# A four-block graph and state-space kernel: tokens by indirect transfers, leaky ReLU by the absolute value, a select by position on GpSimd, a fourth lane

## The chip, the cores and the metric

The kernel runs on one core of one Trainium2 chip. The core has TensorE (PE, with its weight loads shown apart as PEld), VectorE (DVE), ScalarE (ACT), GpSimd (POOL) and SyncE (SP), each with an in-order queue of its own, and 16 DMA engines. The metric is the time of one execution on the device in microseconds; lower is better.

## The reference, cut to what matters

The input x is 64 batches of 256 tokens of 256 features, in float32. Four residual blocks follow each other, each on a layer norm of x. `before` and after compute the same thing.

```
# block 1: two graph attentions (the second under adj), with MLPs between
e   = leaky_relu(f1[:, :, None] + f2[:, None, :], 0.2)
e   = where(adj > 0, e, -9e15)                 # second attention only
h'  = elu(softmax(e) @ h)
# block 2: the 127 tokens of a batch with the largest weight go through an FFN
w         = x @ wr + br
idx       = top_k(w, 128)[:127]
y         = (gelu(x[idx] @ w1 + b1) @ w2 + b2) * w[idx]
x         = x + scatter(y at idx, else 0)      # 'x' on the right: normalized x
# block 3: graph attention under adj, with -inf outside it
# block 4: Mamba-2 over one chunk of 256 positions
L     = exp(cs[l] - cs[s]) for s <= l, else 0  # per head, cs = cumsum(dt * A)
Y     = ((C @ B^T) * L) @ (x * dt), then gate, norm, two projections
```

Block 2 is added to x again after the layer norm, as in each block.

## The kernel before

**Tiling.** A group is two batches: 512 tokens, in four chunks of 128 partitions. There are 32 groups (n). A tile of x for one group is `xt`, 128 x 4 x 256. All matmuls are float32; the trace shows two records for a matmul and one for a transpose.

**Lanes.** The work is written as Python generators that issue a few instructions and then `yield`. Such a generator is a lane: `a` is the first block (`gnn0`, 55 steps), `b` the second and third (`ffn0` and `gnn1`, 57 steps), `c` the fourth (`ffn1`, 87 steps), `d` the second half of the first group's first block, `e` and `f` the two halves of the last group's fourth block (78 steps each), and `w` the preparation of weights. The order of instructions on all engines is that in which the steps are called: L1038 to L1048 walk three strings of letters. `FIRST` starts the pipeline, `ORDER` is walked 29 times, each pass taking one lane `a`, one `b` and one `c` of different groups through all its steps, and `LAST` empties it. A letter whose lane may not begin yet does nothing (`is_there`, L1021); what is left after `LAST` is stepped in turn (L1046 to L1048). `e` and `f` may begin when all groups have passed `b`.

**scores** (L422) turns f1 and f2 into unnormalized attention. f2 is spread over the partitions by four transposes into PSUM (`fb`), the row maximum gives the shift `nm`, ScalarE computes leaky ReLU by `Prelu` with f1 as bias, four instructions of 128x256, then `Exp` with the shift as bias and the row sum accumulated in `den`. VectorE takes the reciprocal and GpSimd scales e (L473). `turned` (L476) then transposes e on TensorE. It is called three times per group.

**Token choice** (L597). `wc` is each token's weight. `wrow` spreads it over the partitions, and two VectorE instructions per chunk count the larger ones (`tie`), which is the token's `rank`. `pick` (L628) is a 0/1 matrix of 128 tokens by 128 ranks. TensorE selects the tokens by multiplying with it (`psel`, L635), transposes it (`pt`, L645) and, after the FFN, brings the result back by multiplying with its transpose (`po`, L695). VectorE adds it to xn with the weight wc (L702), GpSimd adds that to xt (L705).

**The decay matrix** (L805 to L826). A row of cs goes through DRAM (`csd`) and is spread over 128 partitions by a DMA of SP into E (L809). E has 384 columns for each batch: the first 256 positions against the first 128, and the last 128 against the last 128; the first and the third 128 are the blocks on the diagonal (`diag`). For each head VectorE takes the minimum with cs of the partition (L820), which makes everything above the diagonal exp(0) = 1, ScalarE takes the exponential (L826), and VectorE multiplies by `cb` (L899), which is C B^T times `tri3` (L891), ones on and below the diagonal and zeros above. So the zeros come from tri3.

**Other names in the prediction.** `pp`, `pz`, `ph`, `py`, `u`, `pa`, `pd`, `pn`, `pb`, `pss`, `pst`, `pr` are PSUM tiles of the matmuls in the lanes; all PSUM tiles share eight buffers (L235). `mm` (L251) and `tr` (L254) are helpers, so nearly all TensorE records have one of these two lines. The convolution is one ScalarE and three VectorE instructions per 128 channels (L841, L845), followed by tanh and a product (`silu`, L850, L851). `power` (L264) is the inverse root of the variance on GpSimd.

Of the kernel before, what the change touches and what calls it, by code (L numbers as in the profile page):

```python
# [8 lines left out]
F32 = mybir.dt.float32  # L9
I32 = mybir.dt.int32  # L10
BF16 = mybir.dt.bfloat16
# [10 lines left out]
    "dwddadadwaaadawdaaddadaddaaaaadddaaddaaaaddaddaddadaaadaddaddwawdaaaaaaadddadddawdaaaaadadaadaddbaba"  # L22
    "aaabaaaabbaawaaaabwaabaaaaababbbaabbbwababababbbbabaaaabaabaawabababbaaaaabbbaaabbbbabbbaababbababab"
    "baababbbaaaabbabbbabbbaaacwccaababcaababbaabcaaabaaabacabbabbbbbaaabaabaabcbcabaabwbbaacabbaabawabca"
    "bbbab"
)
ORDER = (
    "cAaaccbbbbbbacabaccccbccaabacccabcbccabaacbccacabcaaaacacacbcccccbcacabcccbcaaacacbbccccccacaaccbcac"
    "cbacacabccabcccbcbBabccaccbcccabbcacaacbaccacbcbaacbcbbcbcababcbbcbCccbbbbaacaacabcaabbcbbabbbbbccc"
)  # L30
LAST = (
    "ececefefceecbbceccbbcbffbbbccfcbbfceccebbfcccbefccbcbeceebfcccecccecccceccfbccbcecccbccbeeccbefceccf"
    "ccccccfeeebbccecccfecffffcccfbffebcccbfbceffbccbcccefebbcefcccfceeebcbccccbfefccbcccbfbffcbbccccbcbb"
    "cfceefcbfbbcfefcbbcffbfecccbfcbfefbbbfbfbccffeeeebffbeccccfffebbfebbefbecfcbccccccbcbbcbffcccbeeceec"
    "ebfecbbbbcebffcceccbccccbeccebccececbbefcccffecfccffccfecfebcebceeceecebcffbcfeccfffcfecfeccefcececc"
    "cfe"
# [4 lines left out]
def kernel(ctx: ExitStack, tc: tile.TileContext, a: dict, out: bass.AP):  # L41
# [52 lines left out]
    tri3 = cons("tri3", P, 3 * P)  # L94
    nc.gpsimd.memset(tri3, 1.0)
    for blk in (0, 2):
        nc.gpsimd.affine_select(
            out=tri3[:, blk * P : (blk + 1) * P],
            in_=tri3[:, blk * P : (blk + 1) * P],
            compare_op=ALU.is_ge,  # L100
            fill=0.0,
            base=0,
            pattern=[[1, P]],
            channel_multiplier=-1,
        )

# [13 lines left out]
    ranks = cons("ranks", P, P)  # L120
    with tc.tile_pool(name="first", bufs=1) as first:
        iota_i = first.tile([P, P], I32, tag="iota_i", name="iota_i")
        nc.gpsimd.iota(iota_i, pattern=[[1, P]], base=0, channel_multiplier=0)
        nc.vector.tensor_copy(ranks, iota_i)
    nc.vector.memset(ranks[:, KK:P], -1.0)
# [75 lines left out]
    for t, ap in ((dtb, a["L1_ffn_dt_bias"]), (negA, a["L1_ffn_A_log"])):  # L201
# [28 lines left out]
        "xn": 2, "pk": 3, "v": 2, "g": 4,  # L230
# [6 lines left out]
    def tiled(pool, shape, tag, name, bufs):  # L237
        return pool.tile(list(shape), F32, tag=tag, name=name, bufs=bufs)
# [4 lines left out]
    def sm(tag, *shape, bufs=4):  # L243
        return tiled(small, shape, tag, tag, bufs)

    def sized_sm(tag, n, most, *rest, bufs=4):

        return sm(tag, P, most, *rest, bufs=bufs)[:, :n]
# [39 lines left out]
    def made_ready():  # L288
# [19 lines left out]
        nc.vector.tensor_scalar(mask1, adj, 0.0, -1e37, ALU.is_le, ALU.mult)  # L308
# [31 lines left out]
        yield  # L340
        for t in (b1h, conv_w, conv_b, W_in[:, :, :DI]):
            nc.vector.tensor_scalar(t, t, 0.5, None, ALU.mult)
# [23 lines left out]
    def sized(G, own=None):  # L366
# [12 lines left out]
        def columns(tag, name, most=512):  # L379
            t = wide(lambda tag, name: t512(tag, name) if most == 512 else tiled(t2, (P, most), tag, name, 4), tag, name)  # L380
            return t[:, (own or 0) * N : (own or 0) * N + T]
# [40 lines left out]
        def scores(f1, f2, mask, strict, tag):  # L422
# [3 lines left out]

            yield
            fb = psum("fb")
            for c in range(C):
                tr(fb[:, tok(c)], f2(c).to_broadcast([P, P]), ident)  # L430
            halves = [slice(h * N, (h + 1) * N) for h in range(2)]
            es = [t512(tag, "e") for b in range(G)]
            rows = [fb[:, b * N : (b + 1) * N] for b in range(G)]
            top = sized_sm("top", C, 4)
            if mask is None:
                most = sized_sm("most", G, 2)
                nc.vector.tensor_reduce(most, fb[:, :T].rearrange("p (b j) -> p b j", b=G), AX.X, ALU.max)
                for c in range(C):
                    nc.vector.tensor_scalar(
                        top[:, c : c + 1], most[:, c // 2 : c // 2 + 1], f1(c), -1.0, ALU.add, ALU.mult  # L440
                    )
            else:
                most = sized_sm("topm", C, 4)
                for c in range(C):
                    e = es[c // 2][:, halves[c % 2]]
                    nc.vector.tensor_tensor_reduce(
                        e, rows[c // 2], mask[:, c % 2, :], 1.0, -3e38, ALU.add, ALU.max, most[:, c : c + 1]
                    )
                for c in range(C):
                    nc.vector.tensor_scalar(  # L450
                        top[:, c : c + 1], most[:, c : c + 1], f1(c), -1.0, ALU.add, ALU.mult
                    )
            yield
            nm = sized_sm("nm", C, 4)
            nc.vector.scalar_tensor_tensor(nm, top, ALPHA, top, ALU.mult, ALU.min)
            den = sized_sm("den", C, 4)
            for c in range(C):
                e = es[c // 2][:, halves[c % 2]]
                nc.scalar.activation(e, rows[c // 2] if mask is None else e, AF.Prelu, bias=f1(c), alpha=ALPHA)
            yield  # L460
            for c in range(C):
                e = es[c // 2][:, halves[c % 2]]
                nc.scalar.activation(e, e, AF.Exp, bias=nm[:, c : c + 1], accum_out=den[:, c : c + 1])
            yield
            if strict:

                nc.vector.scalar_tensor_tensor(den, nm, 1e30, den, ALU.is_lt, ALU.mult)
# [614 lines left out]
```

## Time and profile before

| | us |
|---|---|
| median of 3 runs (lowest, highest) | 3652.24 (3652.19, 3652.80) |
| the profiled execution's own time | 3653.81 |
| its span, first to last instruction | 3652.1 |
| mean granted TensorE clock | 0.99 |
| DMA: bytes moved, share of 16 engines | 150.89 MB, 12.1% |

The page gives busy shares, the span in 40 slices, and groups of instructions; the trace behind it can be asked for stretches of time, for the instructions of one engine in order, and for what a waiting instruction waited for. Since matmuls overlap, the mean duration of one (379 ns for 256 columns) is longer than its share of the time, and a stretch of TensorE work is better read from the start of one group of matmuls to the start of the next. Groups that the change touches:

| line, engine | what, per instruction | count | mean ns |
|---|---|---|---|
| L820 DVE | minimum of E's diagonal blocks, 128x512 | 248 | 885 |
| L899 DVE | E times cb, 128x768 | 248 | 988 |
| L891 DVE | cb times tri3, 128x384 | 64 | 547 |
| L628 DVE | pick, 128x128 | 128 | 297 |
| L439, L450 DVE | top, 128x1 | 384 | 205 to 207 |
| L455 DVE | nm, 128x4 | 94 | 157 |
| L459 ACT | Prelu, 128x256 | 384 | 475 to 526 |
| L463 ACT | Exp with sum, 128x256 | 384 | 516 |
| L473 POOL | e times 1/den, 128x256 | 384 | 505 |
| L702 DVE | result of the FFN times wc plus xn, from PSUM, 128x256 | 128 | 476 |
| L715 DVE | two-input product in SBUF, 128x256 | 256 | 423 |
| L97 POOL | select by position, 128x128, once per block | 2 | 296 |

### The profile page before, as it was taken

To read this page: it belongs to the slowest core of one execution; us is meant where nothing else is said; L and a number is where in the kernel's file an instruction comes from. 1 tells how busy PE (TensorE), PEld (TensorE's weight loads), DVE (VectorE), ACT (ScalarE), POOL (GpSimd) and SP (SyncE) were. 2 spreads that over 40 slices of the span, in tenths; PEclk is the share of its full clock that TensorE was granted. 3 is DMA by queue.
4 is the path that set the end of the run, shared out by engine and by line. 5 is a ranking of instruction groups with operands and counts; after the bars stand their busy time and mean duration, and the time that the engine had idled before them with its cause. 6 is when DMAs were issued, how large, how long until landed. Compare 5 with 4: busy or idle time off the path is not lost.

```text
span 3652.1 us, 50662 instructions
## 1 busy us (share of the span) xinstructions
PE 3533.4 (97%) x17004; PEld 2550.6 (70%) x17004; DVE 2842.1 (78%) x7275; ACT 2189.1 (60%) x4942; POOL 1146.8 (31%) x1274
## 2 busy tenths in 40 slices
PE   8999999999999999999999999999999999999876
PEld 6766776776776776776776776776776777776544
DVE  5577778777778777878777878777878777878776
ACT  4565665665665665666665666655666655666544
POOL 2223333323333323333323333323333323333222
PEclk9999999999999999999999999999999999999989
DMA  3011101111101111101111101111101111101111
GB/s 116 1 39 43 49 15 43 48 42 46 49 15 43 48 40 48 49 15 43 48 40 49 48 16 43 49 40 49 44 20 43 48 40 49 41 23 37 43 43 48
DMA packets 90260, 150.89 MB, mean 41 GB/s; under 512 B 12304, under 2 KB 57232, under 8 KB 90000
## 3 DMA queue, kind: packets, MB, share of 16 engines
q1 hardware_dynamic: 90000, 147.65, 12.1%
q8 instruction: 135, 2.21, 0.2%
q14 instruction: 125, 1.02, 0.1%
HBM read 125.86 MB, written 17.56 MB: 39 GB/s over the span
## 4 chain that ended last, share of the span: by engine, by line
PE 81%; DVE 12%; ACT 4%; issue 1%; POOL 1%; DMA 1%; SPq 0%; ACTq 0%; POOLq 0%; DVEq 0%
PE pp L251 31%; PE u L251 10%; PE py L251 9%; PE po L251 7%; PE pz L251 6%; PE pt L254 5%; PE ph L251 4%; PE pa L251 3%; PE psel L251 2%; DVE st L393 1%; DVE xt L595 1%; DVE g L674 1%; DVE w L498 1%; DVE g L671 1%; DVE w L594 1%; PE pss L251 1%
## 5 line engine op out<-in xcount | busy, mean ns | idle before, releaser
L251 PE MATMUL pp<-W_fc,o 128*128 128x256 f32 (+1 forms) x2048 | 460.1, 379 | 0.4 <-DVE W_fc L286 0.4
L845 DVE SCALAR_TENSOR_TENSOR xs<-pp,conv_w,xs 128x510 f32<-128x510 f32 (+5 forms) x495 | 359.9, 728 | 93.9 <-ACT xs L841 79.9
L251 PEld LDWEIGHTS pp<-W_fc,o 128*128 128x128 f32 x2048 | 381.9, 189 | 67.8 <-issue 15.9
L826 ACT ACTIVATE E<-E,ncs 128x256 f32<-128x256 f32 (+1 forms) x1024 | 382.0, 449 | 61.0 <-DVE E L820 58.3
L473 POOL TENSOR_SCALAR e<-e,den 128x256 f32<-128x256 f32 x384 | 186.8, 505 | 714.2 <-PE pp L251 350.3
L251 PE MATMUL pp<-xT,W_in 128*128 128x512 f32 (+1 forms) x660 | 303.6, 593 | 0.0
L850 ACT ACTIVATE th<-xs 128x512 f32<-128x512 f32 (+1 forms) x165 | 101.7, 617 | 326.6 <-DVE xs L845 311.4
L925 POOL TENSOR_TENSOR xs<-xs,gz 128x512 f32<-128x512 f32 (+1 forms) x132 | 205.9, 1561 | 203.0 <-DVE xs L924 200.5
L251 PE MATMUL py<-w,g 128*128 128x256 f32 x1024 | 236.2, 383 | 20.7 <-DVE g L674 20.7
L899 DVE TENSOR_TENSOR E<-E,cb 128x768 f32<-128x768 f32 (+1 forms) x264 | 250.5, 964 | 1.1
L705 POOL TENSOR_TENSOR xt<-xn,xt 128x512 f32<-128x512 f32 x64 | 81.3, 1270 | 526.1 <-DVE xn L702 525.9
L251 PE MATMUL pz<-xT,W_in 128*128 128x512 f32 (+1 forms) x528 | 242.8, 583 | 0.0
L567 POOL TENSOR_TENSOR o<-w,o 128x512 f32<-128x512 f32 (+1 forms) x132 | 180.7, 1369 | 197.8 <-DVE w L501 197.8
L251 PE MATMUL ph<-sel,w 128*128 128x256 f32 x1024 | 242.0, 379 | 0.0
L251 PE MATMUL po<-W_ol,xs 128*128 128x256 f32 x1024 | 241.3, 379 | 0.0
L251 PEld LDWEIGHTS py<-w,g 128*128 128x128 f32 x1024 | 190.0, 190 | 70.9 <-DVE g L674 46.7
L251 PE MATMUL pp<-xT,mlp_w 128*128 128x512 f32 (+1 forms) x528 | 236.5, 583 | 0.7 <-ACT xT L419 0.7
L251 PE MATMUL u<-at,h 128*128 128x256 f32 x1024 | 236.8, 379 | 0.0
L251 PE MATMUL pp<-o,mlp_w 128*128 128x512 f32 (+1 forms) x528 | 231.1, 590 | 2.9 <-POOL o L567 2.9
L820 DVE TENSOR_TENSOR E<-E,ccs 128x512 f32<-128x512 f32 (+1 forms) x264 | 224.3, 863 | 0.0
L393 DVE BATCH_NORM_STATS2 st<-xt 128x6 f32<-128x256 f32 x512 | 185.1, 413 | 49.7 <-POOL xt L750 23.4
L251 PEld LDWEIGHTS u<-at,h 128*128 128x128 f32 x1024 | 191.7, 190 | 37.6 <-issue 7.3
(179 smaller groups left out, 7722.3 us busy)
## 6 DMA issues: line engine op xcount, KB each, us to landing
E<-csd SPq DMA_DIRECT2D x248, 384.0 KB
xt<-in_x_dram SPq DMA_DIRECT2D x31, 512.0 KB
out_dram<-xt SPq DMA_DIRECT2D x31, 512.0 KB
cs<-xs SPq DMA_DIRECT2D x64, 64.0 KB
E<-csd SPq DMA_DIRECT2D x16, 192.0 KB
w<-in_L_ffn_w_dram SPq DMA_DIRECT2D x2, 1024.0 KB
W_in<-in_L_ffn_W_in_dram SPq DMA_DIRECT2D x1, 1160.0 KB
mlp_w<-in_L_gnn_mlp_w_dram SPq DMA_DIRECT2D x2, 512.0 KB
```

The source lines that it names most:

```text
L251: nc.tensor.matmul(to, lhsT, rhs, start=start, stop=stop)
L254: nc.tensor.transpose(to, of, eye)
L393: nc.vector.bn_stats(st[:, c, :], xt[:, c, :])
L473: nc.gpsimd.tensor_scalar(e, e, den[:, c : c + 1], 1.0, ALU.mult, ALU.mult)
L567: nc.gpsimd.tensor_tensor(o1[m], w, o1[m], ALU.add)
L705: nc.gpsimd.tensor_tensor(pair(xt, b), xn[b], pair(xt, b), ALU.add)
L820: nc.vector.tensor_tensor(diag, diag, ccs[:, :, :, h : h + 1].to_broadcast([P, G, 2, P]), ALU.min)
L826: nc.scalar.activation(e[:, b, to], e[:, b, to], AF.Exp, bias=ncs[:, b, half, h : h + 1])
L845: nc.vector.scalar_tensor_tensor(s3[:, :, d:], p3[:, :, : N - d], conv_w[:, m, 3 - d : 4 - d], s3[:, :, d:], ALU.mult, ALU.add)
L850: nc.scalar.activation(th, s, AF.Tanh)
L899: nc.vector.tensor_tensor(e2, e2, cb2, ALU.mult)
L925: nc.gpsimd.tensor_tensor(yt, yt, gz, ALU.mult)
```

## The change

**Tokens by indirect transfers.** `pick`, its transpose and the three kinds of matmul with it are gone. A new function `ranked_tokens` computes the rank as before, turns it into two columns of integers (`to` is the rank, `back` the rank cut at 127) and lets GpSimd write each chunk of xn to its ranks' rows in DRAM (`sorted_x`, four indirect DMAs per group). SP loads the first 128 rows of each batch (`taken_x`), TensorE transposes them (four transposes), and the FFN runs on them. Its result y is set to zero in row 127 (by `valid`, a column with zero at partition 127, in the instruction that adds b2, and b2 is multiplied by it once), SP writes it to DRAM (`ranked_y`), and four indirect DMAs of GpSimd gather for each token the row of its rank, row 127 for those not chosen.

**A fourth lane.** `ranked_tokens` is the lane `g`, 9 steps; `b` begins after it and has 50 steps. All three strings are new. `FIRST`, `ORDER` and `LAST` have 310, 201 and 407 letters (305, 199 and 403 before); ORDER is still walked 29 times.

**Leaky ReLU by the absolute value.** With s = f1 + f2, leaky_relu(s) = 0.4 (1.5 s + |s|). ScalarE computes |s| with f1 as bias, VectorE adds 1.5 times the row to it in a new instruction per chunk, and Exp applies the scale 0.4 and a shift that contains f1. The top of four chunks is one instruction in place of four. f1 and f2 are copied from PSUM to a tile `f` of their own, in a ScalarE copy of two columns beside that of h.

**The select.** In place of the minimum, GpSimd's affine_select writes -3e38 above the diagonal of E's diagonal blocks, one instruction per batch and head, so that Exp gives zero. tri3 is gone, and cb is a copy.

**Buffers.** `xn` has four instead of two, `row` is a new tag with one, small tiles have three instead of four by default; dt, ccs and ncs have one each.

```diff
+        def ranked_tokens(xt, of):
             xn = yield from layernorm(xt, *of, "xn")
...
-                nc.vector.tensor_scalar(pick[:, c, :], ranks, rank[:, c : c + 1], None, ALU.is_equal)
+            to, back = (tiled(small, (P, 4), t, t, 4, U32)[:, :C] for t in ("to", "back"))
+            nc.vector.tensor_copy(to, rank)
+            nc.vector.tensor_scalar(back, rank, float(KK), None, ALU.min)
+            yield
+            sorted_x = [rowd.tile([N, D], F32, tag=f"sorted{b}", name="sorted") for b in range(G)]
+            for c in range(C):
+                nc.gpsimd.indirect_dma_start(
+                    sorted_x[c // 2], bass.IndirectOffsetOnAxis(ap=to[:, c : c + 1], axis=0), chunk(xn, c), None
+                )
+            yield
+            taken_x = t512("row", "taken")[:, : G * D]
+            for b in range(G):
+                nc.sync.dma_start(taken_x[:, b * D : (b + 1) * D], sorted_x[b][:P, :])
+            return xn, wc, back, taken_x
...
+                    tr(
+                        psel[:, (k * G + b) * P : (k * G + b + 1) * P],
+                        taken_x[:, b * D + k * P : b * D + (k + 1) * P], ident,
+                    )
...
+            ranked_y = [rowd.tile([P, D], F32, tag=f"ranked{b}", name="ranked") for b in range(G)]
             for b in range(G):
-                yield
-                po = psum("po")
...
+                nc.sync.dma_start(ranked_y[b], y[:, b * D : (b + 1) * D])
+            yield
+            ws = [t512("g", "w") for b in range(G)]
+            for c in range(C):
+                nc.gpsimd.indirect_dma_start(
+                    chunk(ws, c), None, ranked_y[c // 2], bass.IndirectOffsetOnAxis(ap=back[:, c : c + 1], axis=0)
+                )
...
+                nc.scalar.activation(size[c // 2][:, halves[c % 2]], rows[c], AF.Abs, bias=f[:, c, 0:1])
+            for c in range(C):
+                e = es[c // 2][:, halves[c % 2]]
+                nc.vector.scalar_tensor_tensor(
+                    e, rows[c], (1 + ALPHA) / (1 - ALPHA), size[c // 2][:, halves[c % 2]], ALU.mult, ALU.add
+                )
...
-                nc.vector.tensor_tensor(
-                    diag, diag, ccs[:, :, :, h : h + 1].to_broadcast([P, G, 2, P]), ALU.min
-                )
+                for b in range(G):
+                    nc.gpsimd.affine_select(
+                        out=diag[:, b], in_=diag[:, b], compare_op=ALU.is_ge, fill=-3e38, base=0,
+                        pattern=[[0, 2], [1, P]], channel_multiplier=-1,
+                    )
...
-                nc.vector.tensor_tensor(cb[:, b, :], pb[b][:, : 3 * P], tri3, ALU.mult)
+                nc.vector.tensor_copy(cb[:, b, :], pb[b][:, : 3 * P])
```

## The prediction

> **What bounds the kernel now.** I read the page's shares first, then the slices, then single stretches.
>
> ```profile
> PE 3533.4 (97%) x17004; PEld 2550.6 (70%) x17004; DVE 2842.1 (78%) x7275; ACT 2189.1 (60%) x4942; POOL 1146.8 (31%) x1274
> ...
> PE   8999999999999999999999999999999999999876
> ...
> PEclk9999999999999999999999999999999999999989
> ```
>
> TensorE is busy 97% of the span, flat from the second slice to the last three; what is lost lies at the ends. The stretches (length, then PE, PEld, DVE, ACT, POOL busy, clock) say it in us:
>
> ```profile
> 1997.00:2106.50 109.50, 108.55 (x529) 78.64 (x528) 87.43 (x224) 67.80 (x153) 35.83 (x39) 1.00 0.12 41
> ...
> 3423.20:3533.00 109.80, 82.88 (x361) 53.49 (x359) 84.72 (x193) 50.92 (x110) 23.36 (x24) 0.88 0.10 36
> 3533.00:3652.10 119.10, 80.48 (x400) 54.82 (x400) 83.41 (x196) 51.91 (x124) 26.54 (x30) 0.87 0.13 44
> ```
>
> In the middle TensorE idles 0.95 us of 109.5; in the last 229 us it idles 65. The chain that ended last shows the period by one burst that recurs:
>
> ```profile
> 1996.73 12.11 PE pp L251 x44
> ...
> 2106.46 12.11 PE pp L251 x44
> ```
>
> 109.73 us per pass of ORDER, which runs 29 times. So a microsecond of TensorE work taken out of a group is worth 32 us, and a microsecond of new stall in a pass costs 29.
>
> **What leaves and enters TensorE.** One period of its timeline (start, us, instruction); a stretch is read from start to next start, since matmuls overlap:
>
> ```profile
> 2055.93 0.60 PE L254 MATMUL wrow<-ident,wc 128*128 128x128 f32 x4
> 2056.36 2.78 PE L251 MATMUL pp<-W_hand,o 128*128 128x258 f32 x12
> ...
> 2063.15 1.95 PE L251 MATMUL psel<-pick,xn 128*128 128x128 f32 x16
> 2064.93 0.60 PE L254 MATMUL pt<-ident,pick 128*128 128x128 f32 x4
> 2065.37 1.89 PE L251 MATMUL po<-W_ol,xs 128*128 128x256 f32 x8
> ...
> 2097.70 1.03 PE L251 MATMUL po<-y,pT 128*128 128x256 f32 x4
> 2098.57 1.88 PE L251 MATMUL pp<-xT,mlp_w 128*128 128x512 f32 x4
> ```
>
> Removed: selection psel 1.78, transposes of pick 0.44, two po of 0.87: 3.96 us. Added: four transposes of taken_x, as wrow's four: 0.43. Net 3.53 per group, times 32 is 113.0: 3652.1 - 113.0 = 3539.1 of span, if every idle microsecond stays. As a check I walked the letters of both ORDERs, giving each step its TensorE time from such rows (eight 256-column records 1.73, four of 512 columns 1.72, four transposes 0.44): 107.5 before (109.73 with stalls and small pieces), 104.1 after.
>
> **The other engines, per group, by the rows' means.** VectorE loses the minimum on E (L820, 8 x 0.885 = 7.1), pick (4 x 0.297 = 1.2), twelve one-column tops and three nm (2.9), and 0.3 on small reads. It gains twelve 128x256 scalar_tensor_tensor in scores, four as L702 (0.476) and eight as L715 (0.423): 5.3; and about 1.9 for top, peak, shift, to and back. Net -4.2 of 87. ScalarE keeps four Abs where it had four Prelu (0.48 to 0.53 either way), gains eight two-column copies (0.2 each by the read of an accumulator, 0.207) and loses pT (0.59): +1.0 of 68. Both stay below TensorE, so this is worth nothing in the middle. By position nothing gets worse either: the largest surplus of queued VectorE work over TensorE work in a stretch is 9.3 us before and 9.1 after. Table set-up, masks, buffer counts and the scan's ones are one-off or free.
>
> **GpSimd and the transfers: not in this trace.** Sixteen selects of 128x256 per group: 0.30 from below (the 128x128 select of L97 took 0.296), 1.0 from above (twice the row below); nearest is the one-input L473 of that shape, so 0.5, 8 us. Eight indirect transfers of 128 rows: from below 0.29, SP's issue of a csd write; from above 3.7 (below); the sum does not hang on the value between, I take X = 1.2. Then GpSimd has 36 + 8 + 10 = 54 of 106 us. The bytes (eight transfers and four plain ones of 128 KB, 1.5 MB on 4.7 MB per group) meet DMA engines that are busy 12%.
>
> The select also puts a wait where there was none: the exp of E on ScalarE, until now behind VectorE, stands behind GpSimd's in-order queue. Behind a waiting exp stand conv's first pass, elu's exps and the copies that empty PSUM. For heads 0 to 3 GpSimd is free (about 7 us of work in 20 us of letters, and E's first load is issued 8.6 us before its select, where the stretches show six loads busying the DMA engines for 9.5 us, 1.6 each). For heads 4 to 7 it is not: from e's first scale to the scatter it has 4 scales of 0.5 twice, four o adds of 1.4, two gatings of 1.6 and eight selects, 16.8 us in 20. ScalarE (65% busy) can lag there by some 2 us, and VectorE's E*cb and the matmuls py behind it; py stands 3 to 8 us later. I charge it to the 0.5 us below.
>
> Do they stand where someone waits? In ORDER the scatter is followed by 17.6 us of TensorE letters before psel. Its path: to and back ready about 0.8 us after the scatter's letter, 4X, landing, SP's two loads, landing. Landing by the csd write and the E reads behind it:
>
> ```profile
> SPq L809 <- DMA csd<-csT: 26.2, 87, 1.1
> ...
> 2088.53 0.29 SPq L787 DMA_DIRECT2D csd<-csT  x1
> 2089.81 2.95 SPq L809 DMA_DIRECT2D E<-csd  x6
> ```
>
> About 1.0 from the end of issue to the released wait; with 128 KB I take 1.5, then 0.8 to issue two loads and 1.6 to land. Sum 4.7 + 4X: hidden up to X = 3.2. While SP waits for the scatter, the next in its queue is the load of x for a later group and the cs transfer, neither due within 20 us. The gather stands 10.7 us behind y; y to landing 0.75 + 0.7 + 1.5, so GpSimd reaches it about 3 us after y and is done 4X later, 8 in all; the VectorE step behind it then waits 0 to 2 us, covered by 12 us of fc0 and pp matmuls. Behind the gather on GpSimd come xt's add, rstd, the select of head 3 and e's scale, due 9 to 16 us later.
>
> **A rule against it.** GpSimd work beside VectorE is in the trace (minimum/median/maximum ns):
>
> ```profile
> L925 POOL TENSOR_TENSOR xs<-xs,gz x132: 725/1657/2666, 272.0 to 3638.1; 128x512 f32<-128x512 f32 x124, 128x256 f32<-128x256 f32 x8
> ...
> L705 POOL TENSOR_TENSOR xt<-xn,xt x64: 1265/1268/1283, 142.1 to 3530.7; 128x512 f32<-128x512 f32 x64
> ...
> L820 DVE TENSOR_TENSOR E<-E,ccs x264: 410/685/1767, 236.9 to 3629.6; 128x512 f32<-128x512 f32 x124, 128x256 f32<-128x256 f32 x8
> ```
>
> A two-input operation of one shape takes 1.27 undisturbed and 1.66 in the crowded stretch; the DVE minimum is held up to 1.1 us. The Trainium skill, SBUF — State Buffer, § SBUF: two separate sides, calls the shared port pair an exclusive lock, under which a GpSimd-issued DMA cannot write its descriptors; § A bandwidth-pool intuition that's wrong gives 620 ns alone and about 3100 under a VectorE copy. No transfer of that sort is in this trace. By the row X grows 0.39, to 1.6: hidden. By the rule it grows 2.5, to 3.7: 4.7 + 14.8 is 1.9 beyond the cover, 29 x 1.9 = 55 us, 3612. I go by the row, since VectorE's operations here are single ones of 0.4 to 1.0 us.
>
> **What I add.** In the first scores the letters leave 7.8 us from fb to the transposes of e, where there were 9.5, and one VectorE step more on the way. 0.5 us per pass for this and GpSimd's in-order queue: 14.5. At the end LAST is worse placed: the last group's scatter has only 2.2 us of TensorE work before psel, against 8.7 or more of path: +7. The last gather chain (y, landing, four gathers, landing, moments, f1, f0, fb: about 19) has 9.5 us of cover; the wait there stood already at
>
> ```profile
> 3538.16 1.78 PE L254 MATMUL fb<-ident,f 128*128 128x128 f32 x4 [6.59 <-DVE junk L715]
> ```
>
> so +3. Ten steps of the last b come after LAST with c's last three as cover: +1. Against it, VectorE is the busier engine there (84.7 of 110) and sheds the minimum: three rounds of about 2.5 us, -8. Sum +3. 3539.1 + 14.5 + 3 = 3556.6; the profiled run took 3653.81 around a span of 3652.1, the median is 3652.24, 0.1 above that span: **3557**.
>
> **Rivals.** *Given back in the scores (3609).* VectorE has about 10 us queued between the last conv and e's scale (xn 0.9, moments 2, most 0.7, silu 0.7, two ln 1.5, the new step 2.2, f1 1.9) for 7.8 us of cover; nothing says it can be early, because xn waits for the gather. 2.3 us per pass, 67 in place of 14.5. For it: the old chain used 8.0 of 9.5. Against: VectorE runs ahead there by TensorE's 7 us of fc0. *The indirect transfer is slow (slower than before).* Place: the scatter before psel, which stands first in TensorE's queue. Stall 4(X - 3.2) per pass; it eats the remaining gain of 95 us at X = 4.0 and is slower from there; at X = 5, 29 x 7.1 = 206, 3763. For it: the rule above, and no row. Against: it must be three times my X. *It does less than it says, in the other sense:* the ends gain as much as they lose and the middle keeps its 0.95: 3530 or a little less.
>
> **Numbers.** Forecast (3530 to 3580) 0.52; given back (3580 to 3645) 0.27; slow transfers or another new bound beyond 3660 0.16; within 0.2% (7 us, what a measurement of this kernel tells from nothing) 0.02; below 3530 0.03. Range 3530 to 3645, which holds 0.79. Faster 0.82, same 0.02, slower 0.16.
>
> **What would show it.** The recurring pp burst 106.2 to 107 us apart; psel's transposes taking 0.44 with no idle before them except once near the end; DMA instructions of GpSimd under 3.2 us; E's selects near 0.5; POOL near 50%. I am wrong if psel, e's transposes or pt of xs show a wait in every period, above all if psel's releaser is the transfer to taken.

## The result and the profile after

The changed kernel takes 3634.01 us (median of five runs, 3628.95 to 3636.9) where the kernel before took 3652.45 beside it (3652.19 to 3654.57): ratio 0.9944, 95% interval 0.9932 to 0.9956. It is faster by 18 us, 0.6%, where 95 were predicted. One execution of g1 below took 5930.97 us at a mean granted clock of 0.555 and is left out of its row. The profiled run spans 3632.7 us. From its page: the busy shares, two rows of the slices, and the chain that ended last by engine.

```profile
PE 3461.4 (95%) x16236; PEld 2445.3 (67%) x16236; DVE 2803.0 (77%) x7142; ACT 2190.2 (60%) x5166; POOL 1599.5 (44%) x2040
...
PE   8999999999999999999999999999999999999675
...
PEclk9999999999999999999999999999999999999887
...
PE 47%; DVE 28%; ACT 14%; POOL 5%; issue 4%; DMA 1%; SPq 0%; ACTq 0%; DVEq 0%; POOLq 0%
```

TensorE did lose its work (72 us less busy), and its slices still read 9. But the last row says something new: the chain runs over TensorE for only 47% of the span. The same row before was

```profile
PE 81%; DVE 12%; ACT 4%; issue 1%; POOL 1%; DMA 1%; SPq 0%; ACTq 0%; POOLq 0%; DVEq 0%
```

The period, the time of one pass of ORDER, is read from the recurring pa burst in TensorE's timeline (start, length):

```profile
2008.01 3.72 PE L239 MATMUL pa<-at,xn 128*128 128x256 f32 x16
...
2115.93 3.72 PE L239 MATMUL pa<-at,xn 128*128 128x256 f32 x16
...
2224.04 3.72 PE L239 MATMUL pa<-at,xn 128*128 128x256 f32 x16
```

Over 26 passes the mean is 108.47 us, against 109.73 before. So a pass gained 1.26 us, where 3.03 were predicted (3.53 less 0.5): 29 x 1.77 = 51 us of the miss. What is left of the span besides 29 periods is called the ends. They grew from 469.9 to 487.1, by 17.2, where they were to shrink by 7.6 (three more groups at 3.53, less 3): 25 us. Together these are the 76 us by which the span exceeds the 3556.6 of the sum.

Where does a pass give back? Start to start, summed by the tiles of TensorE's instructions and averaged over those passes, psel and pick fell by 1.72 and po by 1.73: 3.45 in all, as computed. Against that, pn (the transposes of dtT and csT) with the py of the feed-forward block grew by 1.41, and W_fc's products with the transposes of e, which follow each other, by 1.04. The rest nets to 0.26 less, so 2.19 came back. The waits of the steady part name both places (total us, times, longest):

```profile
PE pn L242 <- DVE csT L795: 19.0, 27, 0.8
PE pt L242 <- POOL e L470: 13.1, 48, 0.7
PE pn L242 <- DVE dtT L793: 9.8, 27, 0.4
```

Before, the longest wait there was another, at py:

```profile
PE py L251 <- DVE g L674: 15.2, 27, 0.6
```

The chain of waits of one pass (start, length, what) shows what lies between them:

```profile
2165.83 1.14 PE pd L239 x8
...
2168.39 1.28 ACT L791
2169.68 0.42 ACT dz L791
2170.12 1.28 ACT L682
2171.41 0.64 ACT g L682
2172.07 0.69 DVE g L684
...
2185.13 1.48 ACT E L842 x4
2186.61 0.68 ACT xs L857
2187.31 0.76 DVE xs L861
...
2206.35 1.33 DVE e L451 x4
...
2209.62 1.24 POOL e L470 x2
2210.90 0.44 PE pt L242 x2
```

From pd at 2166 to the transposes of e at 2211, 45 of the 108 us, the chain never touches TensorE: softplus, the two table loads (L791 and L682), the convolutions with the exp of E in between, the scores' new step. TensorE is busy through nearly all of it and yet not what the pass waits for. Its idle time says little of this: from 270 to 3190 us it idles 54.3 of 2920 us, and 25.8 before, which is 2.0 and 0.95 per pass.

The new operations themselves came out near their estimates. The rows of the scatter (minimum/median/maximum ns) and of the select (busy us, mean ns, idle time before it):

```profile
L637 POOL DMA_INDIRECT sorted<-xn,to x128: 955/982/1749, 83.2 to 3447.5; - x128
```
```profile
L835 POOL TENSOR_SCALAR_AFFINE_SELECT E<-E 128x256 f32<-128x256 f32 x512 | 225.4, 470 | 104.2 <-DMA E<-csd 102.7 <-PE pt L242 0.4
```

### The profile page after: what moved, and what is told of

It is laid out like the page before. It is cut to its first block, busy times and chain, and to the rows that moved or that the text cites. A ratio compares the mean times of both kernels' runs of the same rounds, so it can differ in the third digit from the quotient of the medians.

```text
span 3632.7 us, 51434 instructions
## 1 busy us (share of the span) xinstructions
PE 3461.4 (95%) x16236; PEld 2445.3 (67%) x16236; DVE 2803.0 (77%) x7142; ACT 2190.2 (60%) x5166; POOL 1599.5 (44%) x2040
## 4 chain that ended last, share of the span: by engine, by line
PE 47%; DVE 28%; ACT 14%; POOL 5%; issue 4%; DMA 1%; SPq 0%; ACTq 0%; DVEq 0%; POOLq 0%
PE pp L239 9%; DVE xs L861 9%; PE u L239 9%; PE po L239 6%; PE py L239 5%; PE pz L239 4%; PE ph L239 4%; ACT E L842 4%; POOL e L470 3%; PE pa L239 3%; PE pt L242 3%; DVE xn L395 3%; DVE junk L729 2%; DVE st L383 2%; ACT xs L857 2%
## 5 line engine op out<-in xcount | busy, mean ns | idle before, releaser
L239 PEld LDWEIGHTS pp<-W_fc,o 128*128 128x128 f32 x2048 | 383.3, 190 | 67.4 <-issue 12.8
L470 POOL TENSOR_SCALAR e<-e,den 128x256 f32<-128x256 f32 x384 | 225.4, 604 | 351.8 <-DVE den L467 171.5
L567 POOL TENSOR_TENSOR o<-w,o 128x512 f32<-128x512 f32 (+1 forms) x132 | 170.4, 1293 | 241.6 <-DVE w L498 241.6
L835 POOL TENSOR_SCALAR_AFFINE_SELECT E<-E 128x256 f32<-128x256 f32 x512 | 225.4, 470 | 104.2 <-DMA E<-csd 102.7
L239 PE MATMUL po<-W_ol,xs 128*128 128x256 f32 x1024 | 232.7, 381 | 0.0
L496 ACT ACTIVATE w<-w,neg 128x512 f32<-128x512 f32 (+1 forms) x196 | 139.9, 714 | 152.2 <-DVE w L495 152.1
L679 POOL TENSOR_SCALAR g<-g 128x512 f32<-128x512 f32 x128 | 91.5, 715 | 316.8 <-ACT g L678 312.0
L395 DVE TENSOR_SCALAR xn<-xt,mv,rstd 128x256 f32<-128x256 f32 x512 | 222.7, 491 | 5.6 <-POOL rstd L255 4.9
```

The source lines that it names most:

```text
L239: nc.tensor.matmul(to, lhsT, rhs, start=start, stop=stop)
L395: nc.vector.tensor_scalar(chunk(xn, c), xt[:, c, :], mv[:, c, 0:1], rstd[:, c : c + 1], ALU.subtract, ALU.mult)
L470: nc.gpsimd.tensor_scalar(e, e, den[:, c : c + 1], 1.0, ALU.mult, ALU.mult)
L496: nc.scalar.activation(w, w, AF.Exp, bias=neg1)
L567: nc.gpsimd.tensor_tensor(o1[m], w, o1[m], ALU.add)
L835: nc.gpsimd.affine_select(out=diag[:, b], in_=diag[:, b], compare_op=ALU.is_ge, fill=-3e38, base=0, pattern=[[0, 2], [1, P]], channel_mult ...
```

## The experiments

The times are medians beside runs of the kernel before on the same chip; the period is the mean distance of the pa bursts over 26 passes, the ends are the profiled span less 29 periods.

| run | us | ratio to before, 95% | period | ends |
|---|---|---|---|---|
| before | 3652.45 | 1 | 109.73 | 469.9 |
| the change | 3634.01 | 0.9944 (0.9932 to 0.9956) | 108.47 | 487.1 |
| e1_pn | 3639.99 | 0.9965 (0.9953 to 0.9978) | 108.61 | 486.8 |
| e2_turned | 3707.09 | 1.0148 (1.0131 to 1.0165) | 110.93 | 489.8 |
| e3_linear | 3604.37 | 0.9871 (0.9855 to 0.9888) | 107.54 | 482.2 |
| e4_min | 3867.68 | 1.0586 (1.0568 to 1.0603) | 116.30 | 497.3 |
| e5_scores | 3645.72 | 0.9977 (0.9967 to 0.9987) | 108.82 | 488.2 |
| e6_pd | 3748.63 | 1.0254 (1.0237 to 1.0271) | 112.68 | 488.3 |
| e7_exp | 3615.25 | 0.9890 (0.9874 to 0.9907) | 107.97 | 483.5 |
| e8_last | 3655.27 | 1.0001 (0.9991 to 1.0011) | 108.49 | 513.1 |
| f1_halfpo | 3626.76 | 0.9926 (0.9909 to 0.9943) | 108.29 | 483.8 |
| f2_halfmlp | 3662.38 | 1.0022 (1.0010 to 1.0033) | 109.45 | 488.9 |
| f3_softplus | 3700.96 | 1.0130 (1.0113 to 1.0147) | 110.81 | 485.3 |
| v1_exp_softplus | 3664.46 | 1.0027 (1.0017 to 1.0036) | 109.78 | 478.8 |
| g1_before_halfpo | 3620.96 | 0.9911 (0.9891 to 0.9930) | 108.60 | 470.3 |
| g2_noselect | 3598.74 | 0.9851 (0.9835 to 0.9867) | 107.65 | 475.0 |
| g3_plain | 3619.20 | 0.9907 (0.9889 to 0.9923) | 108.29 | 477.6 |
| v2_exp_ln | 3628.18 | 0.9929 (0.9913 to 0.9946) | 108.27 | 491.6 |
| h1_all_out | 3578.85 | 0.9788 (0.9772 to 0.9805) | 107.20 | 470.3 |
| v3_order | 3638.48 | 0.9958 (0.9941 to 0.9974) | 108.46 | 490.1 |

**The clock.** In these 26 passes the granted TensorE clock is 1.00 before, in the change and in most runs. In some it falls to 0.50 for 3.4 us in part of the passes, once in each: e4 (25 of 26), e6 (22), f2 (17), e2 (13), f3 (9), v1 (3), e1 (1). That costs time of its own. In f2, such a stretch, a pass with it and the pass after it without (length, PE, PEld, DVE, ACT, POOL busy, clock):

```profile
2013.80:2017.10 3.30, 3.12 (x16) 3.10 (x16) 3.10 (x14) 1.13 (x4) 1.38 (x3) 0.50 0.00 0
1918.78:2028.64 109.86, 105.07 (x498) 74.90 (x496) 86.82 (x220) 67.68 (x160) 49.54 (x64) 0.98 0.17 55
2028.64:2136.94 108.30, 103.55 (x498) 73.37 (x496) 86.38 (x220) 67.67 (x160) 49.75 (x64) 1.00 0.17 56
```

The ends are not longer for the clock: over the last 219 us it is 0.87 before and 0.84 after, but also 0.84 in h1, whose ends are as short as before.

Theory 1 was that the new ORDER leaves too little TensorE work beside two chains, a fault of a few letters at each; its rival, theory 2, that GpSimd's added work holds the others up.

**Two waits taken by themselves.** e1 begins ORDER with `bAbcccc` in place of `cbAbccc`; e2 moves a's steps 21 and 22:

```
- c33 a20 a21 b38 c34 a22 b39 c35 c36 b40 c37 c38 b41 c39 c40 a23
+ c33 a20 b38 c34 c35 c36 a21 c37 c38 a22 b39 c39 c40 b40 b41 a23
```

> The changed kernel with one letter of ORDER moved: the transposes of dtT and csT (pn) come two of b's py letters later (1.7 us of TensorE work), nothing else. Theory 1 (the new ORDER leaves too little TensorE work at two places; the new operations themselves are hidden): the wait of pn, about 1.25 us per pass with the exposed weight load, goes; 29 x 1.25 = 36 us, so 3598, between 3592 and 3612. Theory 2 (GpSimd's selects and transfers hold up the other engines, by their queue or by the SBUF ports, so that a wait taken away at pn turns up at the next letter): 3625 to 3640. If pn's wait is gone but the time of theory 2 is measured, the period's other waits must have grown by as much.

> The changed kernel with two letters of ORDER moved: the transposes of e in the first scores (a's steps 21 and 22) stand behind fb of f and two of the transposes to xs (1.3 us of TensorE work more before the first, 0.9 before the second); the exp and scale of b's scores keep their order among themselves. Theory 1: e's waits of 1.04 us per pass go but for 0.1; 29 x 0.9 = 27, so 3607, between 3600 and 3618. Theory 2: the scale on GpSimd is late whatever the letters are, or the scores of b, whose Abs now stands behind two copies more, take over the wait: 3625 to 3645.

e1 came out at the edge of theory 2's range, and as that theory had it the wait turned up at the next letter; but it is not GpSimd that holds it. The waits of pn are gone, and this row stands in their place:

```profile
PE py L239 <- DVE g L684: 37.6, 27, 1.4
```

The same 1.4 us per pass, one letter on: the third feed-forward block's tanh queues on ScalarE behind softplus and both table loads, and its g on VectorE, behind the scan, then waits 0.2 us more for the tanh. e2 missed both theories. The first scores' wait is gone (W_fc's products are back at 13.88 us per pass, as before), and the second scores, whose Abs now came later, wait in their stead, `PE pt` for `POOL e` 52.0 us in 76 waits where there were 13.1 in 48. That is not all of its loss of 2.46 per pass: its passes with the halved clock take 111.94 on average, the others 109.92.

**Each addition undone or left out.** e3 takes the scores' new form away (without the negative slope), e4 brings the minimum back in place of the select:

```
-                nc.scalar.activation(size..., rows[c], AF.Abs, bias=f[:, c, 0:1])
-                nc.vector.scalar_tensor_tensor(e, rows[c], ..., size..., ALU.mult, ALU.add)
+                nc.scalar.activation(e, rows[c], AF.Identity, bias=f[:, c, 0:1])
```
```
-                    nc.gpsimd.affine_select(out=diag[:, b], in_=diag[:, b], ...)
+                nc.vector.tensor_tensor(diag, diag, ccs[...].to_broadcast([P, G, 2, P]), ALU.min)
```

> The changed kernel with the leaky ReLU's new form taken out of all three scores: one Identity per chunk into e in place of Abs and the scalar_tensor_tensor on VectorE, and Exp with the bias -top; it computes the softmax of the scores without the negative slope. The chain from fb to e's transposes loses a VectorE step of four (1.41 us for the group) and a hop; VectorE loses 5.3 us per group. Theory 1: e's waits in the first scores (1.04 per pass) go, pn keeps its own: 3634 - 30 = 3604, and a few us more from the end, where VectorE chains are exposed: 3592 to 3610. Theory 2 (the scale is held by GpSimd, not by the chain before it): 3622 to 3636.

> The changed kernel with the select alone undone: the minimum on VectorE on E and the multiplication of cb with the triangle are back (VectorE +7 us per group), GpSimd loses its sixteen selects (7.5 us per group). Theory 1 (the select is hidden, and VectorE's relief is worth nothing in the passes): the passes stay within 0.5 us each, the end loses or gains a few: 3628 to 3655. Theory 2 (the selects in GpSimd's queue hold up the exp of E, e's scale and what follows): faster by 0.7 us per pass or more, 3580 to 3615.

e3 came out as theory 1 had it: e's waits vanish, 0.93 us per pass. e4 upset both: 6.6 us of minima per group on VectorE (its busy time grows by 4.7 us per pass) cost 7.8 us per pass, 234 in all. Up to 1.7 of the 7.8 is the clock (3.4 us at half); the one pass without that took 115.25 us, the others 116.35. Its waits stand all along the VectorE stretch:

```profile
PE pt L255 <- POOL e L483: 60.0, 32, 2.4
PE pt L255 <- DVE xs L878: 39.6, 25, 1.9
PE py L252 <- DVE E L926: 29.3, 50, 0.9
```

VectorE is busy 77% of the changed kernel's span and has, in this ORDER, little to give. Theory 3 was made from this and from the chain above: a pass is a TensorE stretch and a VectorE/ScalarE stretch in a row.

**Order faults looked for along that stretch.** e5 issues a's step 14 before b's xn steps; e6 puts the second aggregation behind pd; e7 changes where the exp of E for heads 0 to 3 is issued; e8 has another LAST.

```
e5 - a13 c29 b34 c30 b35 a14 b36 a15 a16
e5 + a13 c29 a14 b34 c30 b35 a15 a16 b36
e6 - C0 a46 a47 a48 c1 a49 a50 b12 a51 c2 c3 c4 b13 b14 a52 c5 b15 a53 c6
e6 + C0 c1 c2 b11 a46 a47 a48 a49 b12 c3 c4 a50 b13 b14 c5 b15 c6 a51
e7 - pp(m) conv(m) silu(m) select(m) exp(m) pp(m+1) conv(m+1) silu(m+1)
e7 + pp(m) conv(m) silu(m) select(m) pp(m+1) conv(m+1) exp(m) silu(m+1)
```

> The changed kernel with three letters of ORDER moved: in the first scores the step with Abs and the scalar_tensor_tensor (a's 14) is issued before b's two xn steps on VectorE (1.56 us), and the reciprocal and scale (a's 16) before b's first dot products (f1); TensorE's letters stand as they were. Theory 3 (the path that sets a pass runs over VectorE and ScalarE, in their queues' order, from pd to the transposes of e: 45 of its 108 us): e is ready 1.5 us earlier, the waits of e's transposes (1.04 per pass) go, and nothing else waits, since TensorE's next need of the xn steps, fb of f, comes after the same sum of VectorE work; 3634 - 30 = 3604, between 3598 and 3614. Theory 2 (the scale on GpSimd is late of itself): 3628 to 3638. A third way, f late: fb of f waits for what e's transposes waited for, 3625 to 3645.

> The changed kernel with ORDER's letters around pd moved: xn, its transposes and pd of the last stage come before the second aggregation (u, 1.73 us of TensorE), which now covers the softplus chain (exp, a table load of 1.28, ln, the scan); the elu steps behind it move along. Theory 3: pn and py stall because that chain of 5 us, and the tanh of g behind the second table load on ScalarE, have 3.5 us of TensorE work beside them; with 5.2 the waits of pn and py go (1.3 per pass) and the VectorE path behind them starts as much earlier: 3634 - 38 = 3596, between 3590 and 3610. Rival (VectorE's work from there to e is a sum that can't start earlier, so the wait turns up at e's transposes, as pn's did at py): 3622 to 3640.

> The changed kernel with the exp of E for heads 0 to 3 issued behind the next convolution's first pass on ScalarE instead of ahead of it; the letters stand as they were. In the trace VectorE waits 1.36 us twice per pass for that first pass behind an exp of 1.48. Theory 3: these 2.7 us lie on the path from pd to e's transposes, so e's waits (1.04 per pass) go, 3604, between 3598 and 3616. Theory 1 (each wait of TensorE is local: pn by the softplus, e by the chain from fb alone): e's chain starts with fb, whose VectorE step is early or late by what is queued, and without a queue it still lasts 8 us for 7.1 us of letters: 3626 to 3637.

> The changed kernel with another LAST: the last group's ranking comes early enough that its scatter has 12 us of TensorE work before psel, the middle stage of the last group begins right after the one before it and its steps are spread so that it ends with the last stage of the group before, and e and f begin only then, as before. My account of the end (the new LAST issues the last group's middle stage late: psel waits 5.6 us, ten of its fifty steps are left over when LAST is through, and e and f, which nothing covers, start at 3549): 20 to 45 us faster, 3590 to 3615. Rival (the end is bound by VectorE's own sum, whatever LAST says): 3625 to 3640.

e7 is the one that hit its place. ScalarE's timeline of the changed kernel, then VectorE's, around one convolution:

```profile
2184.60 0.63 ACT L866 ACTIVATE th<-xs 128x512 f32<-128x512 f32 x1 [0.76 <-DVE xs L861]
2185.13 1.48 ACT L842 ACTIVATE E<-E,ncs 128x256 f32<-128x256 f32 x4
2186.51 0.76 ACT L857 ACTIVATE xs<-pp,conv_b,conv_w 128x512 f32<-128x512 f32 x1
```
```profile
2187.31 0.75 DVE L861 SCALAR_TENSOR_TENSOR xs<-pp,conv_w,xs 128x510 f32<-128x510 f32 x1 [1.36 <-ACT xs L857]
```

VectorE stands idle 1.36 us for a pass that queues behind the exp, and the exp behind tanh, so each convolution takes a round of 5.1 us over both engines. In e7's timeline of ScalarE the two have changed places, and its chain of waits goes through the convolutions on TensorE:

```profile
2177.55 0.63 ACT L874 ACTIVATE th<-xs 128x512 f32<-128x512 f32 x1 [0.76 <-DVE xs L866]
2178.08 0.76 ACT L862 ACTIVATE xs<-pp,conv_b,conv_w 128x512 f32<-128x512 f32 x1
2178.74 1.48 ACT L832 ACTIVATE E<-E,ncs 128x256 f32<-128x256 f32 x4
```
```profile
2176.12 18.98 PE pp L239 x60
```

It gives 0.50 per pass and 4 at the ends, 3615, at the far end of theory 3's range: e's reported wait falls to 0.2 per pass, for the second half of e, which still comes 0.6 after the first. It is the fastest version here that computes all that the reference does, ahead of both kernels. e5 only moved the wait, from the first scores to the second (26.1 us in 26 waits). In e6 the aggregation's first step on ScalarE waits 2.64 us for its product and stands ahead of softplus in the queue, so the longest of pn's waits grew from 0.8 to 1.2; py and xn's transposes took 3.2 us per pass more between them, and W_in's products, where most of the halved clock falls, 0.8. e8 brought the ranking forward into a stretch where VectorE is already full, 34.83 of 40 us (start and end, length, then PE, PEld, DVE, ACT, POOL busy, clock):

```profile
3380.00:3420.00 40.00, 16.66 (x65) 9.71 (x63) 34.83 (x99) 13.02 (x32) 11.86 (x15) 0.78 0.15 43
```

TensorE has 16.66 busy there, 20.95 in the changed kernel, and waits up to 8.95 us for xs. My account of the end (psel's wait, the left-over steps) named real idle time, but not what it costs.

**Is TensorE's work worth anything?** If a pass had a TensorE stretch of its own, work taken out of that stretch should come out of the time in full.

```
f1, g1 -                for m in range(KI):
f1, g1 +                for m in (c % 2, c % 2 + 2):
f2     -                for k in range(KD):
f2     +                k = m % 2
```

> The changed kernel with half of the last stage's output product left out (po takes two of its four W_out blocks): 3.46 us of TensorE work less per pass, in the stretch between e's transposes and pd, in which the chain of waits runs over TensorE throughout. Theory 3 (a pass is a TensorE stretch and a VectorE/ScalarE stretch in a row): the whole of it comes out of the time, 29 x 3.46 = 100, 3534, between 3525 and 3550. Rival (TensorE is held everywhere by the other engines, and work taken out of it comes back as waits in any place): less than half, 3585 to 3634.

> The changed kernel with half of the first mlp product left out (one of two blocks of 128 rows of mlp1_w for each column block): 3.44 us of TensorE work less per pass, as much as in the run beside it, but in the stretch of the convolutions, between pd and e's transposes, in which the chain of waits runs over VectorE and ScalarE. Theory 3: next to nothing comes out, the waits of e's transposes and of xs grow by what is taken: 3615 to 3640. Theory 1 (the waits of TensorE are local, at pn and e, and the stretch between has slack): 3534 to 3560.

> The kernel before with half of po left out (two of four W_out blocks), 3.46 us of TensorE work less per pass, 100 in 29. In its trace TensorE idles 0.95 us of 109.5 and the chain of waits runs over TensorE almost throughout. If that makes TensorE the limit, as I predicted, 3552, between 3540 and 3570. Theory 4 (the other queues, in their fixed order, form a loop that is nearly as long as TensorE's sum, which the profile of before cannot show because TensorE fills every gap): less than half comes out, 3600 to 3650.

f1 fells theory 3 too: 3.46 us of TensorE work out of a pass bring 0.18. The row that takes it back is

```profile
PE u L239 <- ACT at L486: 73.2, 54, 1.6
```

po was what covered the second scores. Start to start, the transposes of e grow by 2.05 and the aggregation by 1.33, which is 3.38 of the 3.46. f2 gets nothing for its cut (W_fc's products, which are followed by the wait for e, take 3.18 more) and even loses 0.98 per pass. That loss is the clock's: the 17 passes with the halved stretch take 109.95 on average, the nine without it 108.51, nearly the change's own 108.47. And g1 shows that this is no property of the change: in the kernel before, whose TensorE idles 0.95 us in 109.5, the same cut brings 1.13 of 3.46, a third. Its first and last pa burst of the 26 passes:

```profile
273.91 1.89 PE L251 MATMUL pa<-at,xn 128*128 128x256 f32 x8
...
3097.52 1.67 PE L251 MATMUL pa<-at,xn 128*128 128x256 f32 x7
```

The change brought 1.26 of 3.45. This is what theory 4 says: the other queues, in their fixed order, form loops nearly as long as TensorE's sum. No run takes such a loop apart.

**What the additions cost.** The select left out, the transfers made plain ones on SyncE, and both with e3 at once:

```
g2 -                    nc.gpsimd.affine_select(out=diag[:, b], ...)
g3 -                nc.gpsimd.indirect_dma_start(...)
g3 +                nc.sync.dma_start(sorted_x[c // 2][c % 2 * P : (c % 2 + 1) * P, :], chunk(xn, c))
g3 +                nc.sync.dma_start(chunk(ws, c), ranked_y[c // 2])
```

> The changed kernel with the select on E left out and nothing in its place, and exp(E) taken without its bias so that it stays in range; the masking of decays is missing from the output. GpSimd loses 7.5 us per pass. If the select is hidden, as I predicted, 3622 to 3636 (some us at the end, where ScalarE waits for it). If it stands on the pass's path through ScalarE, 3605 or less.

> The changed kernel with its eight indirect transfers per group replaced by plain ones of the same size issued by SyncE, so that the tokens go out and come back unsorted; GpSimd loses 7.8 us per pass. If the transfers are hidden, as I predicted, 3626 to 3640. If GpSimd's queue or its transfers hold the pass, 3610 or less.

> The changed kernel with three things left out at once: the leaky ReLU's new form (one Identity, linear scores), the select on E (and exp(E)'s bias), and the indirect addressing (plain transfers by SyncE). TensorE's work and the order of letters are those of the changed kernel. If the three costs add up, 3634 - 30 - 35 - 15 = 3554, the predicted 3557. If the first two stand in the same wait (e's transposes), 3565 to 3590. pn's wait of 1.37 per pass (40 us) stays in either case.

The select is not hidden. ScalarE's timeline of the changed kernel has the exp of heads 6 and 7 behind it, as the prediction feared for heads 4 to 7:

```profile
2130.11 2.88 ACT L842 ACTIVATE E<-E,ncs 128x256 f32<-128x256 f32 x8 [3.67 <-POOL E L835]
```

Without it a pass is 0.82 shorter and the ends 12. That is an upper bound for the select, because the exp without its bias also takes 0.408 us in place of 0.497, 2.8 us of ScalarE per group. The transfers cost 0.18 per pass and 9.5 at the ends, most of it at the start: the third pa burst of the run comes at 263.9 in place of 270.9. All three out give 55 us, not the 80 of their sum: e3 and g2 each take away the same wait, e's. The ends are then 470.3, back at what they were before the change. In h1 a pass takes 107.20, and the chain is TensorE's again:

```profile
PE 78%; ACT 9%; DVE 8%; POOL 3%; issue 1%; DMA 0%; POOLq 0%; SPq 0%; ACTq 0%; DVEq 0%
```

h1 is to be held against the sum that charges nothing for additions, 3539.1. Its span of 3579.1 is 40 us above that: 1.0 per pass and 11 at the ends. The growth at pn and py, 1.41 per pass, is still there in full; other places give 0.4 of it back.

**The softplus chain.** Three more orders were tried on it; f3, and v1 together with e7's, issue softplus ahead of the aggregation that e6 put behind pd, v2 and v3 (both with e7's) part it. f3 and v1 begin ORDER at another letter, so FIRST and LAST change with it:

```
f3, v1 + C0 c1 c2 b11 a46 b12 b13 b14 a47 c3 c4 a48 c5 a49 a50 b15 c6 a51
v2     + c4 b13 b14 a52 c5(exp) b15(tanh) a53 b16 c6(ln, scan) b17 b18 b19 a54 b20 b21 b22 b23 A0 b24 c7(pn)
v3     + b17 b18 b19 b20 b21 a54 b22 b23 A0 b24 c7
```

> The changed kernel with the same rearrangement around pd as in the run that moved the second aggregation behind pd, mended: dtT's softplus is issued ahead of that aggregation, whose first copy held it on ScalarE, v and the square of the third feed-forward block stand ahead of the transposes of xn, and the second pr comes after the third py. 5.2 us of TensorE work between pd and pn, 3.5 before. Theory 3 with the local waits: those of pn and py go, 1.0 to 1.4 per pass, 3593 to 3608, unless e's transposes take over a part of it (up to 3620). If TensorE is held by VectorE's sum between pd and e, 3630 or more.

> The run beside it (softplus covered) together with the exp of E behind the next convolution's first pass, which took 19 us alone (3615). If both waits are local, the two add up: 3634 - 19 - 35 = 3580, between 3572 and 3592. If the second is only what is left when the first goes, 3600 to 3615.

> The changed kernel with the exp of E behind the next convolution's first pass (3615 alone), and the softplus parted: its exp stays, its ln moves behind the tanh of the third feed-forward block, which then needs no table load before it and no longer waits for two; g of that block comes ahead of the scan on VectorE, and pn two py letters later. Theory: the waits at pn fall from 1.37 per pass to 0.5: 3615 - 25 = 3590, between 3582 and 3600. If another chain is next at once, 3605 to 3620.

> The version with the exp moved and the softplus parted (3628), with one letter more moved: the moments of the first stage (1.8 us of VectorE) come behind g of the last feed-forward block instead of ahead of it. If py's wait of 0.9 per pass was that order, 3628 - 26 = 3602, between 3595 and 3610; if VectorE's later work is then late in turn, 3620 or more.

None of the four reached what was hoped for; f3 and v3 fell in the ranges of their rivals. f3 cut pn's 1.01 to 0.68, and xn's transposes took 0.87 more and py 1.38 more. v1 shows e7's part again (1.03 per pass below f3, up to 0.4 of it from fewer passes with the halved clock) on top of the same loss. In v2 pd to the next W_in products took 6.5 us in place of 7.2, then py waited 0.9 for the last block's g. v3 took that wait away, and xn's transposes waited instead, 2.93 in place of 2.15.

## Why the prediction was wrong

**The step that failed** is the sum "3652.1 - 113.0 = 3539.1 of span, if every idle microsecond stays", and with it the price of 32 us for a microsecond of TensorE work per group; **the charge for what is added**, 14.5 us in the passes, was too small besides. The work was counted right (3.45 measured, 3.53 forecast). h1 parts the 76 us. With the additions out, 40 us of the 113 still do not come out: 2.53 of 3.45 per pass, and 11 us at the ends. With the additions in, another 54 us are lost, 1.27 per pass and 17 at the ends, where 17.5 were charged (14.5, and 3 at the ends). The 54 are an upper bound, because h1 also frees the exp of its bias (2.8 us of ScalarE per group); so the 40 are a lower one.

**Why the price failed.** A busy TensorE in an ORDER like this also covers the other engines' chains, and where less of it stands beside them they show. f1 has it plainest: 3.46 us taken out behind e's transposes came back at these and at the aggregation u, and the cut brought 0.18. In the kernel before (g1) the same cut brought a third. The evidence was the idle 0.95 us of 109.5, which does not say how far behind the next chain is; for g1's cut it was about 1 us. In the change, most of the 40 us stand at pn and py, 1.41 per pass. None of the removed matmuls stood there: it is the new ORDER that leaves 3.5 us of TensorE letters from pd to pn, 5.2 before, beside a chain of about 5 us through softplus. The prediction had compared sums of queued work by position ("By position nothing gets worse") and not this chain with its letters. More letters for pn alone are no cure (e1), so what an order must do to be rid of it stays open.

The Trainium skill, Perfetto Trace Analysis, § Identifying the Most-Contended Engine, has the engine with the highest occupancy optimized first, and for TensorE judges the headroom by the share of peak FLOPs and the busy share of weight loads, not by that of matmuls. Weight loads were busy 70% and matmuls 97% here before. Neither tells what a microsecond is worth; g1 does.

**The charge of "0.5 us per pass"** was the guard for the scores and GpSimd's queue, where 1.27 are lost. Most of it stands at W_fc and e's transposes (1.04 above the kernel before), where the prediction had looked (7.8 us of cover for 9.5). That 3634 lies in the band of the rival "given back in the scores" is in part luck: the rival put 2.3 us per pass at that place, and less than half of it is there.

**"Worth nothing in the middle"**, of VectorE's relief, was wrong in the sense that mattered. With the minimum back, the new ORDER takes 3868: it is laid out for the lighter VectorE. The relief was smaller than summed, too: VectorE's busy time per pass fell from 87.67 to 86.45 us, by 1.2 and not by 4.2. The instructions that go and come were sized right; but those that stay grew, most of all the sixteen xn of the layer norms, from a mean of 0.408 to 0.491 us.

**The select** at 0.5 us was right (0.47 mean), its place was foreseen ("behind a waiting exp stand conv's first pass"), and its charge, inside the 0.5, was not: at most 0.82 per pass in g2. e7 got 0.50 by letting conv's first pass go ahead of the exp.

**The transfers** were right: 0.98 us in the median against 1.2, psel with 0.50 in place of 0.44, no steady wait. With the waits between them a group's four scatters take 8.3 us, not 4X = 4.8; that is still below the 12.8 that the forecast had as cover. The rival of the slow transfer falls, and so does the figure of 3.7 that the lock was to give: the longest of the 128 scatters held GpSimd 1.75 us, beside a VectorE that was busy throughout. Whether a lock is behind the 1.62 us that the first scatter of a group takes no run here shows.

**The ends**: psel's waits there are 5.6 us, 7 were forecast. The sum of +3 failed on the relief of 8, which did not show, and on what the additions take where nothing covers them, 17 us by h1.

**Not shown**: that some order of the same letters reaches TensorE's sum. Of ten orders tried nine missed; the runs show several chains within a microsecond of each other, each of which takes over when one is mended. No order was searched for as a whole.

## What to carry to other kernels

An engine that is busy 99% of a loop is the bound only as far as the next chain lies behind it. Measure that distance before pricing work by it: leave out a piece of that engine's work in the kernel as it is and see how much of it comes out of the time. When work leaves an engine whose queue was arranged by hand, look for the chains that this work covered, each with its latency against the work left beside it, and for in-order queues where a long operation that nobody needs yet (the exp of E) stands before a short one that the other engine waits for.

## What was not expected of the hardware

In this program a second scatter into the same DRAM tile is not issued before the first has landed: GpSimd idled 105.8 us before 61 of the scatters for that, 1.7 us each, so a group's four take about 8 us and not 4. The two table loads of a pass took 1.28 us each, and the activation after each began 0.01 us later.
